# A scan and mixture-of-experts layer on one core: another order for the work ahead of the first scan

## The chip, the cores and the metric

The kernel runs on one core of a Trainium2 chip. A core has five engines that each work through their own list of instructions in order: TensorE (PE in the profile, with its weight loads as PEld), VectorE (DVE), ScalarE (ACT), GpSimd (POOL) and SyncE (SP, which here only issues DMAs). They meet through semaphores. Plain DMAs are issued by SP, DMAs with an index list (gathers and scatters) by POOL; both sorts run on the same 16 DMA engines, from two queues.

The metric is the device time of one execution in microseconds. The time before the change is the median of nine executions.

## The reference, cut to what matters

`x` is (2, 2048, 256): B = 2 batches of L = 2048 tokens with D = 256 values. Each token is normalised, and the output is the input plus two results on the normalised tokens:

```python
xn = _layernorm(x)
out = x + scan(xn, ...) + experts(xn, ...)

# scan: tokens of a batch are put in the order of their bucket (8 buckets), then a selective scan
buckets = argmax(l2norm(xn) @ l2norm(means).T)        # (2, 2048)
xs = xn in the stable order of buckets
delta = softplus(dt(x_proj(xs)) + bias); B, C from x_proj(xs) (+ a prompt of the bucket)
h = exp(delta * A) * h + delta * u * B                # 16 states for each of 256 channels
y = (h * C).sum(states) + D * u;  back to the old order

# experts: 8 experts with 256 -> 512 -> 256, each token goes to its two best
logits = xn @ w_gate; top two, softmax of the two: probs
out = sum over the two of probs * ((silu(xn @ w1[e]) * (xn @ w3[e])) @ w2[e])
```

All is float32.

## The kernel before, in words

**Front (lines 134 to 613).** Eight blocks of 512 tokens (`xts`) are loaded; ScalarE, TensorE and VectorE compute their statistics and their scores against the 8 bucket means and the 8 expert gates. `normalize` (L419) normalises each block in place and stores it into `xn_d` in DRAM, with four spare columns a row. `begin_sums` (L911) copies blocks of x into `acc_d`, the DRAM sum of the result (`acc<-in_x_dram`, 512 KB each). `choose` (L512) finds the two best experts of each token; `route` (L531) numbers the (token, expert) pairs by expert and cuts them into NT = 71 tiles of 128. To turn "pair to slot" into "slot to token" it calls `list_tokens` (L305): eight columns, each with two comparisons on VectorE (`one`, `num`), a product on VectorE and one on ScalarE, and 8 matmuls (L337) that add into one PSUM tile `pl`. A list `between` of closures is called after the columns: before the change `find_weights` (L569) after the second and `find_shares` (L589) after the fourth. `find_weights` computes which expert's weights each tile needs (`w_row`) and issues four weight fetches on POOL (tiles 0 and 1: `w13` of 1 MB and `w2` of 512 KB each). `find_shares` computes what each token gives to its two experts and stores that in the spare columns of `xn_d` in two DMAs of 2,048 runs of 16 bytes. From `pl` comes `token_of` (L613), the token of each slot; `load_rows` (L847) then gathers a tile's 128 tokens from `xn_d` (`xg_sb<-xn,token_of`). It waits for all stores to `xn_d`, those of the shares too.

**Sort (L437 to L497).** `sort_tokens` finds each token's bucket, counts with a scan, two triangular and ones matmuls (L462 to L465) and so on, and gives each token its place `pos` in the sorted order; it also finds where each bucket begins and ends (`first`, `last`, by way of the matmul `po`, L482). `list_rows` (L499) turns `pos` into `line_of` with `list_tokens` of two columns. `small_weights` (L273) prepares `diag`, `cp` (by the matmul `pc`) and `na`. When `front.close()` has freed the front's memory, tile 2's weights get a place there (`w13_2`, `w2_2`) and are fetched.

**Pieces and steps.** The scan of a batch goes in four pieces of 512 sorted tokens, eight in all. A piece gathers its rows on POOL (`gather`, `xs<-xn,line_of`, four gathers), transposes them (`turn`), projects them (`project`, `end_projection`: matmuls `px`), stores B and C and loads them back broadcast (`load_b`, `load_z`), finds the step size (`step_size`: matmul `pd`, then three ScalarE activations) and a softplus by four factors (`square` on ScalarE and `series` on VectorE, called for all i by `first_series` in the first piece). A step is four states of half the channels: four products (`bu`, L766) and four scans (`hs`, L775) on VectorE, the decays (`da`) on ScalarE, then transposes and small matmuls on TensorE. There are 64 steps.

**Expert parts.** A tile's work is cut in three parts, `part_up(t, 0)`, `part_up(t, 1)` (16 matmuls each, L875) and `part_down(t)` (8 matmuls, L898, then a scatter-add on POOL): 213 parts. `silu` and `gate` are the tile's VectorE work; they are written two places after their part. `turn` (L854) transposes a tile's rows and computes `own`, the token's share (L862, L866).

**The order** of each engine's instructions is that of the text: the last lines tie each instruction to the one before on its engine. `lead` (L1000) is the hand-written order until the first scan: with each of its 13 entries goes one expert part and then the entry's links of the first piece's chain. From there a planner gives out parts between the steps: each of VectorE's and TensorE's works has a cost, and a part is given when TensorE's sum falls behind VectorE's times one ratio, so that the parts end 16 scans ahead of the last. At the end `out_dram<-acc` copies the sum and the last piece is added to it.

Of the kernel before, what the change touches and what calls it, by code (L numbers as in the profile page):

```python
# [40 lines left out]
F32 = mybir.dt.float32  # L41
# [8 lines left out]
P = 128  # L50
# [12 lines left out]
def scan_moe_kernel(  # L63
# [373 lines left out]
    def sort_tokens():  # L437

        sc = sml.tile([P, BJ, K], F32, tag="sc", name="sc")
        for b in range(B):  # L440
            nc.vector.tensor_tensor(
                sc[:, b * J : (b + 1) * J, :], of_batch(b)[:, :, 0:K],
                m_scale.unsqueeze(1).to_broadcast([P, J, K]), ALU.mult,
            )
        bm = sml.tile([P, BJ], F32, tag="bm", name="bm")
        bk = sml.tile([P, BJ], F32, tag="bk", name="bk")
        first_of_max(sc, bm, bk)
        oh = sml.tile([P, BK, J], F32, tag="both", name="oh")
        nc.vector.tensor_tensor(
            oh.rearrange("p (b k) j -> p b k j", b=B), idx_m.rearrange("p (b k) j -> p b k j", b=B),  # L450
            bk.rearrange("p (b j) -> p b j", b=B).unsqueeze(2).to_broadcast([P, B, K, J]),
            ALU.is_equal,
        )
        cum = sml.tile([P, BK, J], F32, tag="cum2", name="cum")
        nc.vector.tensor_tensor_scan(
            cum.rearrange("p k j -> p (k j)"), keep.rearrange("p k j -> p (k j)"),
            oh.rearrange("p k j -> p (k j)"), 0.0, ALU.mult, ALU.add,
        )
        tot = sml.tile([P, BK], F32, tag="tot", name="tot")
        nc.vector.tensor_copy(tot, cum[:, :, J - 1])  # L460
        pn = ps_m.tile([P, 2 * BK + B], F32, tag="m", name="pn")
        nc.tensor.matmul(pn[:, 0:BK], lhsT=before, rhs=tot, start=True, stop=True)  # L462
        nc.tensor.matmul(pn[:, BK : 2 * BK], lhsT=ones, rhs=tot, start=True, stop=True)
        for b in range(B):
            nc.tensor.matmul(  # L465
                pn[0:K, 2 * BK + b : 2 * BK + b + 1], lhsT=tot[:, b * K : (b + 1) * K],
                rhs=ones[:, 0:1], start=True, stop=True,
            )
        cnt = sml.tile([P, BK], F32, tag="cnt", name="cnt")
        nc.vector.tensor_copy(cnt, pn[:, BK : 2 * BK])  # L470
        base = sml.tile([P, BK], F32, tag="base", name="base")
        for b in range(B):
            own = slice(b * K, (b + 1) * K)
            nc.vector.tensor_tensor_scan(
                base[:, own], ones[:, 0:K], cnt[:, own], 0.0, ALU.mult, ALU.add
            )
        nc.vector.tensor_sub(base, base, cnt)
        nc.vector.scalar_tensor_tensor(base, base, -1.0, pn[:, 0:BK], ALU.add, ALU.add)
        cntT = sml.tile([K, B], F32, tag="cntT", name="cntT")
        nc.vector.tensor_copy(cntT, pn[0:K, 2 * BK : 2 * BK + B])  # L480
        po = ps_m.tile([K, B], F32, tag="m", name="po")
        nc.tensor.matmul(po, lhsT=before[0:K, 0:K], rhs=cntT, start=True, stop=True)  # L482
        fst = sml.tile([K, B], F32, tag="fst", name="fst")
        nc.vector.tensor_copy(fst, po)
        nc.vector.tensor_tensor(cum, cum, over(base, J), ALU.add)
        nc.vector.tensor_mul(cum, cum, oh)
# [443 lines left out]
    for k in range(n_x // 2, n_x):  # L930
        begin_sums(k)
# [46 lines left out]
    def turn_tile(t: int):  # L978
        tiles[t].turn()
        if t + NW < NT:  # L980
            tiles[t + NW].load_rows()
# [187 lines left out]
```

## Time and profile before

| | us |
|---|---|
| median of 9 executions | 795.65 |
| lowest and highest | 792.78 and 796.36 |
| the profiled execution, its own time | 797.61 |
| its span, first to last instruction | 795.8 |

| engine | busy us | share of the span |
|---|---|---|
| PE | 715.5 | 90% |
| DVE | 711.1 | 89% |
| ACT | 508.6 | 64% |
| POOL | 522.2 | 66% |

How to read it: all times of the views are microseconds from the span's start. A timeline row gives the start, the busy time, the engine, the line, the operation, `out<-in`, the size, and in brackets the idle time before it and what is taken to have ended that idle time; rows that follow each other on a line are merged (x7). SPq marks DMA issues of SP. A wait for several semaphores is put down to the last one that the profile shows from an engine, which may not be the real one. PEclk is the granted share of TensorE's clock.

### The profile page before, as it was taken

The page shows a single profiled execution, that of the slowest core. Times are in us where ns is not written, and L with a number is a line of the kernel's source. Part 1 is how long each engine was busy: PE and PEld are TensorE (multiplying, and loading weights), DVE is VectorE, ACT ScalarE, POOL GpSimd, SP SyncE. Part 2 cuts the span into 40 slices and gives each one's busy share as a digit, 9 for nine tenths or more (in the row PEclk, how much of TensorE's full clock was granted, in tenths as well). Part 3 has the DMA queues.
Part 4 walks back from the last instruction along what each step waited for, and adds up shares of the span by engine and source line. Part 5 has one row for each costly group of instructions (what it writes and reads, how often), then busy time and mean ns, then how long its engine had stood idle before and what let it go on. Part 6 is the DMA issues. An engine that isn't in the chain of part 4 may idle for free.

```text
span 795.8 us, 16967 instructions
## 1 busy us (share of the span) xinstructions
PE 715.5 (90%) x6552; PEld 608.3 (76%) x6552; DVE 711.1 (89%) x1162; ACT 508.6 (64%) x986; POOL 522.2 (66%) x374
## 2 busy tenths in 40 slices
PE   7385979899999999899999999999899998999972
PEld 5145768589878998699868986898679886998752
DVE  8866279899999999899989999899799998999991
ACT  4821266585669666776677666866687577766671
POOL 2023738667867786688868886788668887687303
PEclk9656999999999999999999999999999999999986
DMA  9593354754368547664775468537744855444362
GB/s 283 216 321 114 58 172 107 233 157 93 103 157 261 137 107 209 170 171 108 218 189 154 94 214 228 132 57 241 205 109 127 275 162 113 107 105 97 80 218 27
DMA packets 61215, 125.90 MB, mean 158 GB/s; under 512 B 24464, under 2 KB 42032, under 8 KB 53776
## 3 DMA queue, kind: packets, MB, share of 16 engines
q0 software_dynamic: 40224, 65.03, 34.2%
q1 hardware_dynamic: 20912, 59.80, 22.9%
q8 instruction: 52, 0.85, 0.4%
q14 instruction: 27, 0.22, 0.1%
HBM read 180.06 MB, written 27.00 MB: 260 GB/s over the span
## 4 chain that ended last, share of the span: by engine, by line
PE 66%; ACT 6%; DMA 5%; DVE 3%; issue 3%; POOL 2%; POOLq 0%; SPq 0%; ACTq 0%; DVEq 0%
PE p_ps L875 28%; PE py L898 14%; PE pt_s L787 11%; PE y L796 6%; ACT ht L791 2%; DMA out_dram<-acc 2%; PE pt_g L858 2%; PE y L728 1%; PE px L655 1%; DMA xs<-xn,line_of 1%; PE pd L692 1%; DVE hs L775 1%; POOL acc L816 1%; DVE bu L766 1%; DMA acc<-yo,token_of 1%
## 5 line engine op out<-in xcount | busy, mean ns | idle before, releaser
L875 PE MATMUL p_ps<-xT,w 128*128 128x128 f32 x2272 | 281.6, 280 | 5.3 <-ACT sq L702 4.3
L875 PEld LDWEIGHTS p_ps<-xT,w 128*128 128x128 f32 x2272 | 269.7, 195 | 20.2 <-issue 9.2
L775 DVE TENSOR_TENSOR_SCAN hs<-da,carry,bu 128x512 f32<-128x512 f32 x192 | 245.8, 1281 | 0.0
L760 ACT ACTIVATE da<-dl,na 128x512 f32<-128x512 f32 x256 | 182.0, 723 | 1.0 <-DVE hs L775 1.0
L816 POOL DMA_INDIRECT acc<-yo,token_of x71 | 136.0, 1916 | 67.5 <-ACT yo L902 18.5
L766 DVE TENSOR_TENSOR bu<-du,bt 128x512 f32<-128x512 f32 x256 | 173.5, 678 | 0.0
L791 ACT COPY ht<-pt_s 128x512 f32<-128x512 f32 x256 | 137.6, 591 | 33.1 <-PE pt_s L787 32.6
L787 PE MATMUL pt_s<-ident,hs 128*128 128x128 f32 x1024 | 140.5, 283 | 14.2 <-ACT ht L791 8.1
L898 PE MATMUL py<-w,g 128*128 128x256 f32 x568 | 138.0, 386 | 12.2 <-ACT r L696 8.7
L835 POOL DMA_INDIRECT w<-in_w_up_dram,w_row x71 | 94.0, 1324 | 83.2 <-DVE w_row L584 36.7
L787 PEld LDWEIGHTS pt_s<-ident,hs 128*128 128x128 f32 x1024 | 120.0, 145 | 31.2 <-ACT ht L791 15.1
L898 PEld LDWEIGHTS py<-w,g 128*128 128x128 f32 x568 | 103.4, 192 | 26.9 <-ACT r L696 10.3
L849 POOL DMA_INDIRECT xg_sb<-xn,token_of x71 | 91.7, 1291 | 37.7 <-DVE tot L460 16.3
L835 POOL DMA_INDIRECT w<-in_w_down_dram,w_row x71 | 93.7, 1320 | 21.6 <-issue 12.8
L883 ACT ACTIVATE t_sb<-p_ps 128x512 f32<-128x512 f32 x71 | 42.6, 600 | 69.3 <-PE p_ps L875 69.0
L902 ACT ACTIVATE yo<-py,own 128x256 f32<-128x256 f32 x71 | 33.9, 477 | 79.4 <-PE py L898 79.3
L775 DVE TENSOR_TENSOR_SCAN hs<-da,bu 128x512 f32<-128x512 f32 x64 | 78.2, 1222 | 0.0
L796 PE MATMUL y<-ht,z 128*32 128x128 f32 x2048 | 73.5, 277 | 2.5 <-ACT ht L791 1.9
L796 PEld LDWEIGHTS y<-ht,z 128*32 128x32 f32 x2048 | 50.6, 109 | 24.2 <-issue 13.2
L816 POOL DMA_INDIRECT acc<-yt,line_of x28 | 54.7, 1955 | 21.0 <-issue 10.4
L888 DVE SCALAR_TENSOR_TENSOR t_sb<-t_sb,p_ps 128x512 f32<-128x512 f32 x71 | 48.1, 677 | 11.2 <-ACT t_sb L883 10.9
L892 DVE SCALAR_TENSOR_TENSOR g<-t_sb,p_ps 128x512 f32<-128x512 f32 x71 | 48.2, 679 | 9.0 <-PE p_ps L875 6.5
(188 smaller groups left out, 633.0 us busy)
## 6 DMA issues: line engine op xcount, KB each, us to landing
bt<-bc SPq DMA_DIRECT2D x32, 1024.0 KB, 5.2
z<-bc SPq DMA_DIRECT2D x32, 256.0 KB, 3.5
xn<-xt SPq DMA_DIRECT2D x8, 520.0 KB, 2.6
xt<-in_x_dram SPq DMA_DIRECT2D x8, 512.0 KB, 6.9
acc<-in_x_dram SPq DMA_DIRECT2D x8, 512.0 KB, 6.5
w<-in_w_up_dram,w_row POOLq DMA_INDIRECT x71
w<-in_w_down_dram,w_row POOLq DMA_INDIRECT x71
xg_sb<-xn,token_of POOLq DMA_INDIRECT x71
```

The source lines that it names most:

```text
L760: nc.scalar.activation(self.da[i], self.piece.dl[:, self.h, :], AF.Exp, scale=na[:, self.h, n : n + 1])
L766: nc.vector.tensor_mul(self.bu[i], self.piece.du[:, self.h, :], self.piece.bts[self.q][:, i, :])
L775: nc.vector.tensor_tensor_scan(self.hs[:, :, i], self.da[i], self.bu[i], start, ALU.mult, ALU.add)
L787: nc.tensor.transpose(pt[:, j, :], self.hs[:, t0 : t0 + G, :].rearrange("p t n -> p (t n)"), ident)
L791: nc.scalar.copy(self.ht[i], pt)
L796: nc.tensor.matmul(p.ys[self.h][j * G : (j + 1) * G, i, :], lhsT=p.zs[q][:, i * (P // G) + j, :], rhs=self.ht[i][:, j, :], start=False, st ...
L816: ins = nc.gpsimd.indirect_dma_start(out=to, out_offset=bass.IndirectOffsetOnAxis(ap=numbers, axis=0), in_=rows, in_offset=None, compute_o ...
L835: nc.gpsimd.indirect_dma_start(out=to[self.t % NW], out_offset=None, in_=rows, in_offset=bass.IndirectOffsetOnAxis(ap=w_row[:, self.t : se ...
L849: nc.gpsimd.indirect_dma_start(out=self.xg, out_offset=None, in_=xn_d, in_offset=bass.IndirectOffsetOnAxis(ap=token_of[:, self.t : self.t ...
L875: nc.tensor.matmul(p[:, f, :], lhsT=wk[:, h, f * P : (f + 1) * P], rhs=self.xT[:, h, :], start=h == 0, stop=h == ND - 1,)
L892: nc.vector.scalar_tensor_tensor(self.g, self.s, 0.5, self.p3, ALU.mult, ALU.mult)
L898: nc.tensor.matmul(py, lhsT=self.g[:, f, :], rhs=w2[:, f, :], start=f == 0, stop=f == NH - 1)
```

## The change

It moves work in the front and in `lead`; no operation is added or taken away, and all data stay the same.

1. **Shares first.** `find_shares` is called after the list's second column, `find_weights` after the third. The last four `begin_sums` are called behind `route` and `load_rows`, so SP issues the last `xn_d` store and both share stores ahead of them.
2. **Sort in the list.** `sort_tokens` is cut into `choose` (buckets), `count` (counts and matmuls `pn`), `place` (up to `pos`) and `bound` (matmul `po`, then `first` and `last`). `choose` comes after the list's fifth column, `count` after the seventh, `place` after `load_rows`; `list_rows(0)` comes right after the first expert part, and `bound`, `small_weights`, `front.close()` and the fetches of tile 2's weights behind it. `own` (now `find_share`) is written after both tiles' transposes.
3. **Lead.** `lead` has 12 entries, so 12 expert parts: the turns, the projection and both step sizes stand together, and the two series are cut in halves.

```diff
@@ route
-            [lambda: None, find_weights, lambda: None, find_shares],
+            [lambda: None, find_shares, find_weights, lambda: None, sort.choose, lambda: None, sort.count],
@@ Sort.bound: the end of what was sort_tokens, without place
+            po = ps_m.tile([K, B], F32, tag="m", name="po")
+            nc.tensor.matmul(po, lhsT=before[0:K, 0:K], rhs=self.cntT, start=True, stop=True)
+            fst = sml.tile([K, B], F32, tag="fst", name="fst")
+            nc.vector.tensor_copy(fst, po)
+            for b in range(B):
+                nc.vector.tensor_scalar(first[b], begins, fst[:, b : b + 1], None, ALU.add)
+                nc.vector.tensor_scalar(last[b], first[b], self.cntT[:, b : b + 1], None, ALU.add)
@@ the order of the front
-    for k in range(n_x // 2, n_x):
-        begin_sums(k)
     route()
     for t in tiles[:NW]:
         t.load_rows()
-    pos = sort_tokens()
-    diag, cp = small_weights()
-    front.close()
...
-    tiles[NW - 1].load_up()
-    tiles[NW - 1].load_down()
+    for k in range(n_x // 2, n_x):
+        begin_sums(k)
+    sort.place()
@@ turn_tile
         tiles[t].turn()
+        if t > 1:
+            tiles[t].find_share()
@@ before lead
-    def first_series(h: int):
-        for i in range(len(LOG1P) + 2):
+    def first_series(h: int, steps):
+        for i in steps:
...
+    tiles[0].find_share()
+    tiles[1].find_share()
+    jobs[0]()
+    list_rows(0)
+    sort.bound()
+    diag, cp = small_weights()
+    front.close()
...
+    tiles[NW - 1].load_up()
+    tiles[NW - 1].load_down()
+    half = len(LOG1P) // 2 + 1
+    early, rest = range(half), range(half, len(LOG1P) + 2)
     lead = [
-        [lambda: list_rows(0, pos)], [p.gather], [], [], [], [lambda: p.turn(0)],
-        [lambda: p.turn(1), p.find_members],
+        [], [p.gather], [], [], [lambda: p.turn(0), lambda: p.turn(1), p.find_members],
         [lambda: p.project(0), lambda: p.project(1), p.end_projection],
-        [lambda: p.load_b(0), *(lambda q=q: p.load_z(q) for q in range(NQ)), lambda: p.step_size(0)],
-        [lambda: p.step_size(1), lambda: first_series(0)], [lambda: first_series(1)],
-        [lambda: p.begin(0), lambda: p.begin(1)], [lambda: p.mask_z(0)],
+        [
+            lambda: p.load_b(0), *(lambda q=q: p.load_z(q) for q in range(NQ)),
+            lambda: p.step_size(0), lambda: p.step_size(1),
+        ],
+        [lambda: first_series(0, early)], [lambda: first_series(0, rest)],
+        [lambda: first_series(1, early)], [lambda: first_series(1, rest), lambda: p.begin(0)],
+        [lambda: p.mask_z(0), lambda: p.begin(1)],
     ]
```

## The prediction

> **What bounds the kernel now.** I read the chain of waits by engine first, then busy time by stage (columns: PE, PEld, DVE, ACT, POOL, granted PE clock, DMA share, GB/s).
>
> ```profile
> PE 66%; ACT 6%; DMA 5%; DVE 3%; issue 3%; POOL 2%; POOLq 0%; SPq 0%; ACTq 0%; DVEq 0%
> ...
> 36.00:64.00 28.00, 17.09 (x65) 9.29 (x65) 20.54 (x57) 9.24 (x17) 4.37 (x4) 0.50 0.82 264
> 64.00:88.00 24.00, 18.75 (x131) 17.66 (x132) 12.50 (x47) 4.19 (x10) 13.32 (x14) 0.76 0.37 117
> 88.00:116.00 28.00, 22.22 (x125) 16.70 (x124) 12.10 (x23) 15.26 (x28) 12.34 (x11) 0.94 0.51 144
> 116.00:752.00 636.00, 612.60 (x5873) 532.74 (x5871) 608.94 (x890) 437.81 (x858) 478.57 (x315) 0.99 0.58 154
> ```
>
> From 116 to 752 both PE and DVE are 96% busy: nothing of that stage changes. So the change is worth how much earlier the first scan starts, less what work of the front is carried past it. Until then a single chain counts: token list, first tile's rows, sort's list, the piece's gather, its links. The timeline shows it, POOL and SP first, then DVE and PE:
>
> ```profile
> 41.99 0.51 SPq L432 DMA_DIRECT2D xn<-xt  x1
> 47.47 8.70 SPq L602 DMA_DIRECT2D xn<-share  x2
> ...
> 64.46 0.97 POOL L849 DMA_INDIRECT xg_sb<-xn,token_of  x1 [16.32 <-DVE tot L460]
> ...
> 70.00 1.00 POOL L835 DMA_INDIRECT w<-in_w_up_dram,w_row  x1 [2.06 <-DVE na L289]
> 71.31 1.01 POOL L835 DMA_INDIRECT w<-in_w_down_dram,w_row  x1 [0.30 <-DVE v L313]
> ...
> 79.66 1.00 POOL L835 DMA_INDIRECT w<-in_w_up_dram,w_row  x1 [4.80 <-PE p_ps L875]
> 80.97 0.95 POOL L620 DMA_INDIRECT xs<-xn,line_of  x1 [0.31 <-issue]
> ```
> ```profile
> 53.64 0.46 DVE L325 TENSOR_TENSOR num<-idx_p,f 128x568 bf16<-128x568 bf16 x1 [2.69 <-DMA xn<-xt]
> ...
> 60.09 0.23 DVE L613 SCALAR_TENSOR_TENSOR token_of<-tokens,none 128x71 int32<-128x71 f32 x1
> ...
> 104.13 0.69 DVE L713 SCALAR_TENSOR_TENSOR dl<-sq,e 128x512 f32<-128x512 f32 x1 [13.77 <-ACT sq L702]
> ```
> ```profile
> 54.95 4.28 PE L337 MATMUL pl<-num,one 128*128 128x142 bf16 x16 [1.36 <-ACT num L331]
> ...
> 109.35 3.53 PE L875 MATMUL p_ps<-xT,w 128*128 128x128 f32 x16 [4.34 <-ACT sq L702]
> ```
>
> The token list is ready at 60.3, yet the first rows' gather goes at 64.46. DVE's `tot` is no operand of it: the real wait is the second share store, begun at 53.6 (the last of the merged 8.70) with 9.9 us to landing, so 63.5. Why 9.9? The packet counts say it: 3,638 packets under 512 B moved between 57 and 60, and 464 in the nine us before, while the weights' 3 MB went. The small runs stand behind the weights.
>
> **Part 1, shares first.** Shares take 1.9 us of DVE (45.43 to 47.35) and now follow column 2: 39.8 to 41.7. Without the copies ahead, the last `xn` store goes at 39.4, after the one before; the stores land about 2 us apart, so near 43.5. The two share stores then need some 3.4 us (4,096 packets at the rate of 57 to 60): landed by about 47, long before the list. The wait for them goes. What is late next is the list itself.
>
> The weights are fetched 3.3 us later (w_row at 45.8; was 42.5) and now beside the last four copies, 2 MB. The copies took 41.3 to 49.8, the weights 48.3 to 58.6 with 0.5 MB of stores. One after the other that is some 17.5 us from 46.5: 64. The first tile's gather is issued before that and its packets come 1.7 us after issue, so this just hides; each us that DMA is slower costs one. [...]
>
> **Part 2, sort between the columns.** DVE has room in the list: a column is 1.45 us of DVE, but 2.13 of PE (4.27 for two). Added are `choose`, 2.3 us (60.24 to 62.55), and `count`, 1.4 (62.58 to 63.94); the stall of 2.69 for a store goes. From 36.8: two columns 39.8, shares 41.7, column 43.2, weights' rows 45.8, two columns 48.7, `choose` 51.0, columns 52.5 and 54.0, `count` 55.3, last column. The sixth column's factors reach PE at 52.9 through ACT; then PE binds: three columns of 2.13 and `pn`, 1.25 (63.99 to 65.2), end at 60.5. From there 1.1 us to the list: 61.6, 1.3 later than now. The gather follows at 61.9 (POOL went 0.3 after `w_row`): **2.5 us earlier** than 64.46. `place` runs beside the gather's 2.8 us and is hidden; without that cover it costs 2.6. The first part and `list_rows` have the same order as before: `line_of` starts at 74.1 instead of 76.6.
>
> **A new wait.** POOL's order is tile 2's two fetches, tile 3's, then the piece's gather. The first waits for `na`, now behind the list: `bound`, `diag`, `cp` and `na` take 2.0 us (68.25 to 69.91 and 0.35 for `fst`), so 76.2. Then 76.3, 77.6, 78.9 and the gather at 80.2. That is only **0.8** ahead of 80.97: POOL takes 1.7 of the 2.5. Queued behind are tile 4's fetch and rows, needed much later.
>
> **Part 3, lead.** The last gather lands 2.75 after its issue (84.73 to 87.48): 86.7. Until `xd` (95.64) stand now a part, the turn, a down part and the projection: 8.2 us. After: the second turn 0.9, one part 2.0, projection 3.0: 5.8. That is **2.4**. From `xd` to the first `sq` 7.7 now; after it a part 2.05, both `pd` 2.2, a down part 2.4 and `yo` 0.5: 7.2, **0.5**. From `sq` to the first scan 13.5 now (103.38 to 116.93). After: 12 series links of 0.76, `gate` twice, `silu`, `own`, `z` (2.9), two `bu` (1.2) and 0.7 to the first link: 13.9 or so, **0.4 lost**. First scan 3.3 earlier, at 113.6.
>
> Carried past it: one `silu`, 0.6 of DVE. On PE the thirteenth part ended at 116.6; it now ends near 114.0. So DVE is 2.7 ahead and PE 2.6.
>
> **Sum:** 2.5 - 1.7 + 2.4 + 0.5 - 0.4 - 0.6 = 2.7, by PE 2.6; I take 2.6. The profiled execution took 797.6, so 795.0; it lies 2.0 above the median, and the median comes to 795.65 - 2.6 = 793.05, say **793.0**.
>
> **Unknown costs.** The trace shows no piece gather behind three fresh fetches: between nothing (POOL's cadence of 1.3 us is all) and 1.6 us (the fetches' 1.5 MB moved 71.7 to 77.1, then the gather's packets); I take nothing, since the last gather is issued after that. Nor a list with `pn` inside: between 1.3 later (taken) and as now.
>
> The clock is the third. Half clock makes a part 3.53 instead of 2.05. In this trace clock changes stand on a grid of 3.41 us; from full clock, a stretch with PE busy 50% or less is followed by half, one with 58% or more is not. PE will idle some 2.4 us before the last gather lands and 2.3 while a `gate` waits behind the series: each between nothing and 1.7. I take nothing, the rows nearest: 102.8 to 106.2 with 58% kept full clock. [...]
>
> **Rivals.** (a) *Nothing to measure*: one or two windows at half clock (1.7 each) or DMA a us slower, 793.9 to 795.7. [...] (b) *More*: list as early as now and POOL's fetches not held by `na` (they need only the front's memory): 1.3 and 1.6 more, 790.1. Against: `na` ended 0.09 ahead of the fetch at 70.00. (c) *Slower*: the planner has one more part to place, and some parts move by half a step. At a piece's border PE already stands once for 3.1 us (`py` at 331, behind ACT's step sizes), then its part runs at half clock (3.46 instead of 1.9): 4.7 together. One such stall more gives 797.7. It decides from the point where a part falls behind the step sizes in PE's order. Against: the parts' places are the same in the second half. (d) The order of the DMAs could fail to free the gather, if the small runs are slow alone too: over 15 us for both stores. The 1,800 a us after the weights speak against it; I give it no chance of its own.
>
> **Chances.** Forecast 0.48 (791.5 to 794), (a) 0.26, (b) 0.12, (c) 0.14. A measurement of this kernel tells about 0.2% from no change, 1.6 us: faster 0.60, same 0.26, slower 0.14. Range 789.8 to 797.2: (b) and nearly all of (a), with the part of (c) that a half stall gives.
>
> **What would show it.** The shares landed before the list ends, and POOL's first row gather right after `token_of`, near 62; the list's end near 61.6; the piece's first gather near 80.2 and right behind three fetches; `xd` near 92.5; the first scan near 113.6. Wrong if the row gather still waits for a DMA, if the clock is half between 85 and 104, or if the scans start 3 us earlier and the end does not follow.

## The result, and the profile after

| | before | after |
|---|---|---|
| median of the runs | 795.25 (31) | 806.12 (10) |
| lowest and highest | 792.52 and 798.35 | 802.12 and 812.27 |
| the profiled execution, its own time | 797.61 | 806.72 |
| its span | 795.8 | 804.6 |
| first scan, last scan | 116.9, 777.3 | 117.0, 786.0 |

The ratio after to before is **1.0147**, 95% interval 1.0127 to 1.0167: 1.5% slower, where 0.3% faster was forecast, and outside the range. Ratios here and below are the record's and leave out executions more than 1.5% above the fastest of their kernel; the two medians of the table alone give 1.0137. The profiled execution of before lies 2.4 above its median, so the profiles show 8.8 of the medians' 10.9. The first scan did not come earlier, and the 256 scans took 8.6 us longer from the first to the last (669.0; before 660.4).

The chain's shares and the busy times by stage, after (columns as before the change: PE, PEld, DVE, ACT, POOL, granted PE clock, DMA share, GB/s):

```profile
PE 68%; ACT 7%; DMA 4%; DVE 3%; issue 3%; POOL 1%; POOLq 0%; SPq 0%; ACTq 0%; DVEq 0%
...
36.00:64.00 28.00, 17.90 (x72) 10.35 (x72) 22.25 (x65) 8.57 (x14) 6.70 (x7) 0.50 0.85 244
64.00:88.00 24.00, 16.85 (x103) 15.05 (x103) 9.37 (x35) 3.60 (x9) 10.49 (x12) 0.72 0.39 130
88.00:116.00 28.00, 24.76 (x137) 19.13 (x138) 11.91 (x22) 14.45 (x26) 13.42 (x11) 0.88 0.47 141
116.00:752.00 636.00, 611.19 (x5792) 531.93 (x5791) 600.54 (x881) 434.34 (x851) 476.19 (x314) 0.98 0.57 152
```

The last row holds the loss. In the same 636 us VectorE got 600.54 of work done where it was 608.94, and PE ran 5,792 matmuls where it was 5,873; PE is as busy as before (611.2 to 612.6), with the clock at half for 30.7 of the 636 us (before 10.2). VectorE waited 13.9 in all for `t_sb` and 12.3 for the squares (before 6.7 and 9.9).

The front after the change, from the timelines of SP and POOL, then of VectorE and PE:

```profile
36.45 2.76 SPq L432 DMA_DIRECT2D xn<-xt  x3
41.31 1.74 SPq L614 DMA_DIRECT2D xn<-share  x2
43.10 3.18 SPq L927 DMA_DIRECT2D acc<-in_x_dram  x4
...
61.09 0.97 POOL L861 DMA_INDIRECT xg_sb<-xn,token_of  x1 [10.07 <-DVE cnt L477]
...
77.57 1.00 POOL L847 DMA_INDIRECT w<-in_w_up_dram,w_row  x1 [8.61 <-DVE cp L280]
78.88 1.01 POOL L847 DMA_INDIRECT w<-in_w_down_dram,w_row  x1 [0.30 <-issue]
80.19 0.99 POOL L847 DMA_INDIRECT w<-in_w_up_dram,w_row  x1 [0.30 <-issue]
81.49 0.96 POOL L632 DMA_INDIRECT xs<-xn,line_of  x1 [0.30 <-issue]
```
```profile
60.58 0.23 DVE L625 SCALAR_TENSOR_TENSOR token_of<-tokens,none 128x71 int32<-128x71 f32 x1
...
104.44 0.69 DVE L725 SCALAR_TENSOR_TENSOR dl<-sq,e 128x512 f32<-128x512 f32 x1 [12.18 <-ACT sq L714]
```
```profile
95.36 1.98 PE L704 MATMUL pd<-xd,dtT 32*128 32x512 f32 x4
97.83 0.63 PE L870 MATMUL pt_g<-ident,xg_sb 128*128 128x128 f32 x2 [0.50 <-ACT r L708]
99.51 3.78 PE L913 MATMUL py<-w,g 128*128 128x256 f32 x8 [1.04 <-ACT r L708]
```

The row gather goes 0.3 behind `token_of`, 3.4 earlier than before (64.46): the wait for the shares is gone. The piece's gather goes at 81.49, later than before (80.97), the fourth of POOL's row behind three fetches. And between the second step size and the first square stands `py`, late and at half clock (3.78 for 8 matmuls; 1.99 at full clock).

Where the scans lose: the distance of the same scan, after less before, is 0.1 at scan 0, 0.6 at scan 12, 7.4 at scan 24, 6.8 at scan 44, 11.2 at scan 52, 13.2 at scan 80, then down to 6.4 at scan 168 and up to 8.7 at the last. Two places. At the first, `list_rows(1)` (the second batch's list of rows, `pl`) is made beside the scans. PE there, before:

```profile
145.50 1.07 PE L655 MATMUL px<-u,xpT 128*64 128x512 f32 x2
146.69 0.65 PE L337 MATMUL pl<-num,one 128*128 128x32 bf16 x8
148.75 0.65 PE L337 MATMUL pl<-num,one 128*128 128x32 bf16 x8 [1.41 <-ACT num L331]
149.22 2.03 PE L875 MATMUL p_ps<-xT,w 128*128 128x128 f32 x16
151.18 1.07 PE L660 MATMUL px<-member,cp 8*64 8x512 f32 x2
```

and after, with VectorE's row that pays for it:

```profile
145.48 1.07 PE L667 MATMUL px<-u,xpT 128*64 128x512 f32 x2
147.00 0.66 PE L337 MATMUL pl<-num,one 128*128 128x32 bf16 x8 [0.45 <-ACT num L331]
149.07 0.64 PE L337 MATMUL pl<-num,one 128*128 128x32 bf16 x8 [1.41 <-ACT num L331]
150.23 0.66 PE L870 MATMUL pt_g<-ident,xg_sb 128*128 128x128 f32 x2 [0.52 <-PE pl L337]
151.35 3.78 PE L913 MATMUL py<-w,g 128*128 128x256 f32 x8 [0.46 <-ACT xT L872]
155.06 1.96 PE L672 MATMUL px<-member,cp 8*64 8x512 f32 x2
156.95 3.78 PE L890 MATMUL p_ps<-xT,w 128*128 128x128 f32 x16
```
```profile
161.40 0.69 DVE L903 SCALAR_TENSOR_TENSOR t_sb<-t_sb,p_ps 128x512 f32<-128x512 f32 x1 [5.00 <-ACT t_sb L898]
```

Behind the list stands a down part (`pt_g`, `py`) where before an up part (`p_ps`) stood. From 149.1 the clock is half for 13.7 us, `py`, `px` and `p_ps` take 3.78, 1.96 and 3.78 (at full clock 1.99, 1.07 and 2.03), and VectorE stands 5.00. The second place is the next piece's step sizes:

```profile
250.06 1.12 PE L704 MATMUL pd<-xd,dtT 32*128 32x512 f32 x2
251.12 1.08 PE L808 MATMUL y<-ht,z 128*32 128x128 f32 x32
252.13 1.12 PE L704 MATMUL pd<-xd,dtT 32*128 32x512 f32 x2
253.18 0.44 PE L870 MATMUL pt_g<-ident,xg_sb 128*128 128x128 f32 x2
256.75 3.78 PE L913 MATMUL py<-w,g 128*128 128x256 f32 x8 [3.13 <-ACT r L708]
```

`py` stands behind both `pd` and waits 3.13 for ScalarE's step sizes, then runs at half clock (3.78). Before, that down part stood between the two `pd` and did not wait:

```profile
241.76 1.12 PE L692 MATMUL pd<-xd,dtT 32*128 32x512 f32 x2
242.81 1.08 PE L796 MATMUL y<-ht,z 128*32 128x128 f32 x32
243.82 0.44 PE L858 MATMUL pt_g<-ident,xg_sb 128*128 128x128 f32 x2
244.24 1.99 PE L898 MATMUL py<-w,g 128*128 128x256 f32 x8
246.24 1.12 PE L692 MATMUL pd<-xd,dtT 32*128 32x512 f32 x2
```

### The profile page after: what moved, and what is told of

Same layout as the page of the kernel before. It is cut to its first block, busy times and chain, and to the rows that moved or that the text cites. A ratio compares the mean times of both kernels' runs of the same rounds, so it can differ in the third digit from the quotient of the medians.

```text
span 804.6 us, 16964 instructions
## 1 busy us (share of the span) xinstructions
PE 723.3 (90%) x6552; PEld 615.2 (76%) x6552; DVE 709.7 (88%) x1162; ACT 508.9 (63%) x986; POOL 525.1 (65%) x374
## 4 chain that ended last, share of the span: by engine, by line
PE 68%; ACT 7%; DMA 4%; DVE 3%; issue 3%; POOL 1%; POOLq 0%; SPq 0%; ACTq 0%; DVEq 0%
PE p_ps L890 28%; PE py L913 15%; PE pt_s L799 12%; PE y L808 6%; DMA out_dram<-acc 2%; PE pt_g L870 2%; ACT ht L803 2%; PE px L667 1%; PE y L740 1%; DVE hs L787 1%; DMA xs<-xn,line_of 1%; ACT da L772 1%; PE px L672 1%; ACT sq L714 1%; ACT e L707 1%
## 5 line engine op out<-in xcount | busy, mean ns | idle before, releaser
L890 PEld LDWEIGHTS p_ps<-xT,w 128*128 128x128 f32 x2272 | 271.2, 196 | 17.9 <-issue 10.5
L828 POOL DMA_INDIRECT acc<-yo,token_of x71 | 138.8, 1955 | 71.7 <-ACT yo L917 35.7
L803 ACT COPY ht<-pt_s 128x512 f32<-128x512 f32 x256 | 137.8, 590 | 32.9 <-PE pt_s L799 32.4
L913 PE MATMUL py<-w,g 128*128 128x256 f32 x568 | 143.0, 397 | 12.9 <-ACT r L708 8.9
L799 PEld LDWEIGHTS pt_s<-ident,hs 128*128 128x128 f32 x1024 | 121.6, 147 | 30.7 <-ACT ht L803 13.1
L913 PEld LDWEIGHTS py<-w,g 128*128 128x128 f32 x568 | 106.7, 198 | 29.3 <-ACT r L708 10.5
L861 POOL DMA_INDIRECT xg_sb<-xn,token_of x71 | 93.4, 1315 | 33.3 <-issue 13.4
L847 POOL DMA_INDIRECT w<-in_w_down_dram,w_row x71 | 91.2, 1285 | 21.6 <-issue 13.4
```

The lines of the kernel that those rows point to most:

```text
L799: nc.tensor.transpose(pt[:, j, :], self.hs[:, t0 : t0 + G, :].rearrange("p t n -> p (t n)"), ident)
L803: nc.scalar.copy(self.ht[i], pt)
L828: ins = nc.gpsimd.indirect_dma_start(out=to, out_offset=bass.IndirectOffsetOnAxis(ap=numbers, axis=0), in_=rows, in_offset=None, compute_o ...
L847: nc.gpsimd.indirect_dma_start(out=to[self.t % NW], out_offset=None, in_=rows, in_offset=bass.IndirectOffsetOnAxis(ap=w_row[:, self.t : se ...
L861: nc.gpsimd.indirect_dma_start(out=self.xg, out_offset=None, in_=xn_d, in_offset=bass.IndirectOffsetOnAxis(ap=token_of[:, self.t : self.t ...
L890: nc.tensor.matmul(p[:, f, :], lhsT=wk[:, h, f * P : (f + 1) * P], rhs=self.xT[:, h, :], start=h == 0, stop=h == ND - 1,)
```

## The experiments

Two theories. **The parts' order**: `lead` has 12 entries in place of 13, so each tile's pattern of up, up, down is one place on beside every later link of a piece's chain. **The front**: what the new front leaves on POOL and the DMA queues is paid for later. The runs came in five groups, each beside the kernel before, which took 793.7 in the first group and 808.9, 806.4, 803.0 and 808.3 in the others, on other chips or at other times (the first and the third on the same chip); so kernels are compared by their ratio to it and not by their times. For each profile I also give two stretches of scans: from scan 8 to scan 24 (the list of the second batch stands there) and from scan 44 to scan 56 (the second piece's step sizes). These can be set beside each other across the groups: e11 below is the kernel before once more, in a group where it takes 806.4, and its two stretches are 47.2 and 32.0 as in the first profile.

**First group: the two parts of the change alone** (before: 793.7).

`e1_thirteen`, the changed kernel with an empty entry at the end of `lead`:

```diff
-        [lambda: p.mask_z(0), lambda: p.begin(1)],
+        [lambda: p.mask_z(0), lambda: p.begin(1)], [],
```

> The changed kernel with a thirteenth expert part before the first scan (one empty entry at the end of lead). Theory 1, the parts' places: with 12 parts ahead, a down part instead of an up part stands beside batch 1's list (147 to 157 in the changed trace) and beside the step sizes (253 to 260), PE idles and drops to half clock. Then this kernel loses that: first scan some 2 us later than the changed kernel's 117.0, but scan 48 no more than 1 us behind the first scan's shift, and 796 to 799 in all. Theory 2, the front itself (what it leaves on the DMAs and POOL) delays the later stage: then it stays at 805 or more.

`e2_twelve`, the kernel before with its last two entries joined:

```diff
-        [lambda: p.begin(0), lambda: p.begin(1)], [lambda: p.mask_z(0)],
+        [lambda: p.begin(0), lambda: p.begin(1), lambda: p.mask_z(0)],
```

> The kernel before with its last two entries of lead joined: 12 parts ahead of the first scan, front untouched. Theory 1: it loses in the stage of the scans as the changed kernel does, some 7 to 9 us there, with a half clock stretch near 150; first scan 1 to 2 us earlier; 801 to 804. Theory 2: 793 to 796, since its front is that of before.

`e3_old_lead`, the changed front with the 13 entries of the kernel before (its first one empty, since the list is made earlier):

```diff
+        [], [p.gather], [], [], [], [lambda: p.turn(0)],
+        [lambda: p.turn(1), p.find_members],
```

> The changed front with the lead of before, 13 parts in the old places. Theory 1: no loss after the first scan. The row gather lands 0.4 us earlier than before and the piece's gather goes 0.5 later than before, so first scan at 117 to 118 and 795 to 797 in all. Theory 2: 803 or more.

`e4_shares`, the kernel before with part 1 alone:

```diff
-            [lambda: None, find_weights, lambda: None, find_shares],
+            [lambda: None, find_shares, find_weights],
...
+    for k in range(n_x // 2, n_x):
+        begin_sums(k)
```

> The kernel before with one part of the change alone: shares after the list's second column, weights after the third, the last four copies behind them; sort and lead as before. The row gather is issued 1 to 3 us earlier than 64.46; but as in the changed trace the copies and weights end near 66 instead of 59, so the first rows land near 66.5 (before 67.2). Theory 1 and 2 differ little here: theory 1 gives 793.5 to 796 (13 parts, at most 1 us won), theory 2, if the later copies are what disturbs the scans, 800 or more.

| | ratio to before (95%) | first scan | scans 8 to 24 | scans 44 to 56 |
|---|---|---|---|---|
| before | 1 | 116.9 | 47.2 | 32.0 |
| after | 1.0147 (1.0127, 1.0167) | 117.0 | 54.3 | 36.7 |
| e1_thirteen | 1.0030 (1.0013, 1.0048) | 115.9 | 47.2 | 32.0 |
| e2_twelve | 1.0163 (1.0115, 1.0211) | 115.4 | 51.1 | 36.3 |
| e3_old_lead | 1.0026 (1.0004, 1.0048) | 115.7 | 47.2 | 32.0 |
| e4_shares | 1.0001 (0.9981, 1.0020) | 115.6 | 47.2 | 32.0 |

The loss goes with the number of parts and not with the front: one empty entry takes away four fifths of it, and the old front with twelve parts has all of it. In e2's profile the first scan comes 1.5 *earlier* than before, and both stalls are there. The front theory falls. The new front is worth 0.2% at most: e4's first scan is 1.4 earlier in the profile, and the interval of its time just holds that; e1 and e3 are 0.3% slower with the first scan 1.0 and 1.2 earlier. Their profiles show no reason for that (e1's profiled execution was its fastest, 793.0); it stays open.

**Second group: the front further, and fifteen parts** (before: 808.9).

`e5_copies_late`, e1 with the last four copies held behind the first tiles' rows:

```diff
+        tc.add_manual_dep(begin_sums(k), tiles[1].turned.name, after, reason="behind the weights")
```

> The version with thirteen parts ahead of the first scan (first scan at 115.9 in its profile), and besides it the last four of the copies that preset the sums, 2 MB, wait for ScalarE's copy of the first transposed rows, so that nothing but the weights' 3 MB stands ahead of the first rows. In the thirteen-part run the rows were issued at 61.2 and landed at 65.0, a microsecond after the weights' last packet at 64.0. Theory 'the rows wait for the 5 MB ahead of them': the weights end near 59 to 60, the rows land 2.0 to 2.8 after their issue (62.5 to 63.5 if the issue stays near 61), the piece's list comes 1.5 to 2 earlier, at about 72.3, and the first scan 1 to 2 earlier; the time is 0.1 to 0.25% below the thirteen-part version's 796.0, so 794 to 795. Rival 'the weights alone bind, the copies cost nothing': rows land within 0.4 of 65, first scan within 0.4 of 115.9, time unchanged.

`e6_gather_first`, e5 with the piece's gather issued at once:

```diff
     list_rows(0)
+    p.gather()
     sort.bound()
```

> The run before with the piece's row gathers issued on GpSimd ahead of bound's work and of the fetches of tile 2's and tile 3's weights, right behind the list of the piece's rows. Theory 'POOL's fetches that wait for na hold the gather': with the list at about 72 to 74 the first gather goes within 0.6 of it instead of 6.0 later (74.02 to 80.02 in the thirteen-part run), the four gathers land by about 79 to 80 and PE's first link comes up to 5 earlier; the first scan 2 to 5 earlier than in the run before. Tile 2's weights come up to 4 later, near 84, which costs nothing if the part that needs them stands behind the turn. Rival 'PE and the clock set the first links': the gathers land earlier, but the copy of the second turn (87.1 in the thirteen-part run) moves by less than 1, and the time stays within 0.2% of the run before.

`e7_squares_first`, e6 with the first squares ahead of the down part:

```diff
-            lambda: p.step_size(0), lambda: p.step_size(1),
+            lambda: p.step_size(0), lambda: p.step_size(1), lambda: first_series(0, early),
```

> The run before, and besides the first half of the series of chunk 0 stands right behind the two step sizes, ahead of the down part that stood between; the series take one place less, and two empty places stand at the end, so that still thirteen parts are ahead of the first scan. Theory 'the way from the projection to the first square is lost to the down part': 10.2 us after, 9.8 with thirteen parts, 7.7 in the order before; now near 4.5 to 6, the first scan 3 to 5 earlier than in the run before, and since the places of the parts are those of before, the end follows in full: 0.4 to 0.6% below the run before, so 787 to 791. Rival 'the front's gain is eaten later': the first scan comes 3 or more earlier but the last scan by less than 1.5.

`e8_fifteen`, the kernel before with two empty entries:

```diff
-        [lambda: p.begin(0), lambda: p.begin(1)], [lambda: p.mask_z(0)],
+        [lambda: p.begin(0), lambda: p.begin(1)], [lambda: p.mask_z(0)], [], [],
```

> The kernel before with two empty places added at the end of the list ahead of the first scan: fifteen parts instead of thirteen; nothing else. A tile's three parts alternate (two up, one down), so fifteen has the order of twelve beside every later link. Theory 'the order of the parts beside the links decides': PE again stands and falls to half clock where a down part takes the place of an up part (near 150 and 255), and the time is 8 or more above before's, counted from the first scan, besides the two parts' own time being moved and not added: 802 or more. Rival 'one part fewer ahead of the scan is what costs, since it must be done beside the scans': two parts more help or cost at most their idle DVE time, first scan 4 later, and the time is within 0.5% of before's or up to 4 above it.

| | ratio to before (95%) | first scan | scans 8 to 24 | scans 44 to 56 |
|---|---|---|---|---|
| e5_copies_late | 0.9940 (0.9902, 0.9978) | 118.2 | 48.5 | 32.0 |
| e6_gather_first | 0.9854 (0.9787, 0.9921) | 115.5 | 53.1 | 32.0 |
| e7_squares_first | 0.9967 (0.9931, 1.0003) | 114.7 | 51.1 | 32.0 |
| e8_fifteen | 1.0050 (1.0009, 1.0090) | 128.4 | 55.8 | 33.8 |

e5: the weights ended at 59.0 and not at 64.0, but the rows were used only 0.7 earlier (`pt_g` at 64.31; e1 64.97): with the weights out, it still took 2.9 us from the gather's issue to the use of its rows. Neither theory's number: under half of the expected gain, and `line_of` came 0.15 earlier. What it is worth in time is not told, since e1 did not run beside it. e6: POOL's rows, from its repeat `e12_gather_again`, show the gather right behind the list (`line_of` at 73.56), six microseconds earlier than in e1:

```profile
74.00 0.95 POOL L632 DMA_INDIRECT xs<-xn,line_of  x1 [6.42 <-DVE fst L504]
...
77.77 0.95 POOL L632 DMA_INDIRECT xs<-xn,line_of  x1 [0.30 <-issue]
79.02 1.01 POOL L847 DMA_INDIRECT w<-in_w_up_dram,w_row  x1 [0.30 <-issue]
```

but PE first has the parts that stand ahead of the turn, and the copy of the turn comes at 85.3 there (e1 87.1): of six microseconds 1.8 arrive. Beside e5, which differs by this edit alone and ran in the same group, e6's gather goes 4.7 earlier (75.14, e5 79.87) and the copy of the turn comes 3.9 earlier (86.44, e5 90.30); but e5 stands in its front for the unexplained reason told at the end, so neither pair gives the edit's price by itself. e7: the first square came at 96.8 (e6 101.6), as expected, yet the scans only 0.8 earlier: cut in halves, the series' second squares stand behind a part's `t_sb` on ScalarE, and from the first square to the first scan it took 17.9 in place of 13.9. e8: fifteen parts lose, 8.6 in scans 8 to 24; since the first scan comes 11 later too, the time does not tell the two theories apart. Its order on PE does at the list: behind it stand `pt_g` and `py` again, as with twelve. At the second place fifteen is not twelve over again: an up part stands between the two `pd`, `py` behind them waits 0.43, and the stretch loses 1.8.

**Third group: the place of the list, and ten parts** (before: 806.4).

`e9_list_moved`, the changed kernel with the second batch's list seven scans later. `e11_list_moved_before` was meant as the control, but it is the kernel before without any edit and is read as that; so the list's later place with thirteen parts was not measured. The edit of e9:

```diff
-    at_place(2, 3, lambda: list_rows(1), 2.5, 4.0)
+    at_place(4, 2, lambda: list_rows(1), 2.5, 4.0)
```

> The changed kernel with one edit: the list of the second batch's rows is made seven scans later (step 4, place 2 in place of step 2, place 3), where by the planner's sums an up part and not a down part is what PE has beside it; still twelve parts ahead of the first scan. Theory 'a link that has a down part beside it stands and drops the clock': PE's row of half clock from 149 is gone, the scans' distance to the kernel before grows by less than 2 from scan 12 to scan 24 (in the changed kernel 0.6 to 6.9), the stall near 255 with both pd ahead of a down part stays (2.8), and the time is 4 to 6 below the changed kernel's: 800 to 802 where before's is 795. Rival 'with twelve parts some link always pays': the stall turns up beside the moved list or another link before scan 32, and the time stays within 2 of the changed kernel's.

> The kernel before with that same edit, the control: thirteen parts ahead of the first scan, and the list of the second batch's rows at step 4, place 2. There the parts beside it are an up part and then a down part, and beside its old place an up part. Theory 'only the neighbour counts': within 0.3% of before. Rival 'the later place is better for any order' (the list's work falls where VectorE has room): 3 or more below before.

`e10_ten`, e7 with whole series and no empty entries:

```diff
+            lambda: p.step_size(0), lambda: p.step_size(1), lambda: first_series(0, every),
+        ],
+        [lambda: first_series(1, every)],
+        [lambda: p.begin(0), lambda: p.begin(1)], [lambda: p.mask_z(0)],
```

> The version with the gathers first and the squares right behind the step sizes, with the two series whole again and no empty places: ten parts ahead of the first scan, the same place in the pattern of three as thirteen. Theory 'the place in the pattern decides, not the number': no stall at the list of the second batch, first scan near 109.5 to 111 (squares at 96.8 and the 13.5 from there that the kernel before takes), and the time within 0.5% of before's or under it: three parts more beside the scans cost PE 6.1, and the scans start 6 to 7 earlier. Rival 'every part fewer ahead of the scan costs': as twelve cost 1.5%, ten cost 3% or more, 815 and up where before's is 795.

> The version with the piece's gathers ahead of the fetches once more, unchanged, because it was measured at 0.985 of before with an interval of 0.979 to 0.992, while the next version, whose first scan came 0.8 earlier, had 0.997. Theory 'the gain is the early first scan's': at most 1.5 from the front, so 0.998 to 1.000 of before. Rival 'the gain is real and lies in the order of the parts beside the first piece': 0.985 to 0.992 again.

| | ratio to before (95%) | first scan | scans 8 to 24 | scans 44 to 56 |
|---|---|---|---|---|
| e11 (before) | 0.9966 (0.9908, 1.0024) | 121.7 | 47.2 | 32.0 |
| e9_list_moved | 1.0061 (1.0018, 1.0104) | 120.7 | 51.2 | 38.3 |
| e10_ten | 0.9886 (0.9809, 0.9963) | 110.5 | 48.0 | 32.4 |
| e12_gather_again | 0.9912 (0.9868, 0.9955) | 114.3 | 53.3 | 32.0 |

e9 lies between. At the old place nothing stands any more, but at the new one VectorE waits 2.88, and the clock is half from 171.5: the rival's picture. Scans 8 to 24 hold the list's own work in either case and take 4.0 more than before's, where the changed kernel takes 7.1 more; the time says the same, 1.0061. The second place stays (38.3), as expected. e10 bears out the pattern: ten parts, three fewer than thirteen, lose nothing at either place, and the first scan comes at 110.5, 13.6 behind the first square. "Every part fewer costs" falls. e12 repeats e6's gain (0.9912, its rival's number); by their profiles it does not come from scans 8 to 24, where both lose.

**Fourth group: a part inside the list** (before: 803.0).

`f1_part_between` gives two parts at the list, the down part ahead of it and the up part between its columns; the other three give one part between the columns (`f2_before_between` in the kernel before, `f3_gather_between` in e6, `f4_ten_between` in e10):

```diff
-    at_place(2, 3, lambda: list_rows(1), 2.5, 4.0)
+    at_place(2, 3, lambda: (give(), list_rows(1, [give])), 2.5, 4.0)
```

> The changed kernel (twelve parts ahead of the first scan); the down part that stood behind the list of the second batch's rows stands ahead of it, and the up part that came next stands between the list's two columns. Theory 'the list's neighbour': PE no longer idles 1.4 between the columns, nor before the down part; the half clock from 149 is gone, the scans' distance to the kernel before grows by less than 2 between scan 12 and scan 24 (changed kernel: 0.6 to 7.4); the time is 4 to 7 below the changed kernel's, 1.006 to 1.010 of before, the rest being the stalls from 253 on. Rival 'the list costs by itself': the distance still grows by 4 or more there and the time stays within 0.3% of the changed kernel's 1.0147.

> The kernel before with one expert part (an up part) between the two columns of the list of the second batch's rows; the control. In its trace PE idles 1.41 between the columns at full clock, and no stall follows. Theory 'the list costs only where the clock drops': within 0.25% of before. Rival 'the columns' gap costs always': 0.3% or more below before.

> The version with the piece's gathers first (measured at 0.985 and 0.991 of before), with an up part between the two columns of the second batch's list. In both its profiles the clock is half after that list (148.6 and 147.4) and the scans lose 5 to 6 between scan 12 and scan 20. Theory: that loss goes, the time is 0.4 to 0.7% below that of the version without, so 0.980 to 0.986 of before. Rival: the loss only moves, 0.988 to 0.992.

> The version with ten parts and the squares first (measured at 0.989), with an up part between the two columns of the second batch's list. In its profile no half clock follows that list, and the scans lose nothing between scan 12 and scan 20. Theory: within 0.3% of 0.989. Rival 'the columns' gap costs always': 0.985 or less.

| | ratio to before (95%) | first scan | scans 8 to 24 | scans 44 to 56 |
|---|---|---|---|---|
| f1_part_between | 1.0109 (1.0010, 1.0208) | 119.6 | 53.9 | 36.6 |
| f2_before_between | 0.9979 (0.9916, 1.0042) | 121.4 | 48.3 | 32.0 |
| f3_gather_between | 0.9917 (0.9877, 0.9957) | 115.9 | 48.6 | 32.0 |
| f4_ten_between | 0.9896 (0.9810, 0.9982) | 110.3 | 49.5 | 32.4 |

f1: with the down part *ahead* of the list the stretch still takes 53.9, now as a wait of 4.68 on VectorE for the list's first column, whose matmuls stand behind `py`. So my theory of the neighbour behind the list looks too narrow, as far as one profile tells: it is of f1's longest execution, 821.6, where the others took 807.3 to 817.1. In f3 the loss of 6 in scans 8 to 24 is down to 1.4, as expected, but the time did not follow: 0.9917, no better than without, and the number of its rival "the loss only moves". The profiles bear the rival out: against before, f3 loses 5.2 between scans 64 and 112, and g1, the same kernel, 5.1 between scans 128 and 160. f2 and f4 differ from the kernels they were made from by less than their intervals.

**Fifth group: the changed kernel and the best front side by side** (before: 808.3).

> The version with the piece's gathers first and an up part between the two columns of the second batch's list, once more, unchanged (0.9917 of before, where before took 803). Theory 'its own front is shorter': where before takes 794, it takes 0.995 to 0.999 of before; where before takes 803 or more, 0.988 to 0.995. Rival 'it only avoids the stand that before has in some calls': where before takes 794, 1.000 or more; 798 by its own time in either case.

> The changed kernel, unchanged, beside the same runs of before. Theory 'twelve parts lose beside the scans, whatever the front': 1.010 to 1.018 of before again, in either case. Rival 'where before stands in its front, the changed kernel's other front makes up for the loss': within 0.5% of before where before takes 803 or more.

g1 took 0.9955 (0.9896 to 1.0014), just above its theory's 0.988 to 0.995, and 804.5 by its own time where the rival had 798: neither is borne out. g2 took **1.0153** (1.0084 to 1.0222), with 53.7 and 38.6 in the two stretches and the same rows (`py` behind both `pd` with a wait of 3.13 at 262.49). So the changed kernel's loss is the same where the kernel before runs slower by itself. Of the versions with the gather first, five measurements (e6, e12, f3, e10, f4) have their interval below 1, and two (e7, g1) touch it; e5, which does not have it first, lies below 1 too. All are from groups where before takes 803 to 809. None ran where before takes 794, and their own times (795.9 to 805.5) are no better than that: that they beat it there is not shown.

## Why the prediction was wrong

**The step that failed first: "nothing of that stage changes".** It set everything beside the scans aside and counted only how early they start. But `lead` hands the planner one part more, and the parts come in a pattern of three. In all fourteen profiles with 13 or 10 parts scans 44 to 56 took 32.0 to 32.4; in all five with 12 (after, e2, e9, f1, g2) 36.3 to 38.6; in the one with 15, 33.8. That much is shown. Half of it the prediction had in its hands: rival (c) named the mechanism, "behind ACT's step sizes", and its price of 4.7; measured, 36.7 less 32.0 is 4.7 (that it agrees to the tenth is luck: over the five profiles with 12 parts it is 4.3 to 6.6). It was given 0.14 on the ground that "the parts' places are the same in the second half". The half that was read, late in the list of parts, does not tell which part stands beside a link in the first pieces. The order of the two kernels on PE beside each `pd` would have told it without a run.

**No rival had the list.** The stretch from scan 8 to 24 cost 7.1 (54.3 less 47.2), more than the other. With 4.7 that makes 11.8; 3.1 of it is made up by the last scan, which leaves the 8.7.

How much the list costs goes with **the clock**. By the half-clock time between scans 8 and 24, in all twenty profiles: with none the stretch took 47.2 to 48.3; with 3.4 us 48.5 to 51.1; with 6.8 us 51.2; with 10.2 us 53.7 and 53.9; with 13.7 us 53.1 to 55.8.

The prediction's edge, half clock at 50% and full at 58%, was right for the trace it was read from and did not hold beyond it. On the grid of 3.41 us, counted from each profile's own half-clock stretches (after's from 60 to 700 us begin 0, 7, 22, 53, 145 and 177 steps of 3.41 behind 74.05), this is PE's busy share in the window that holds the gap between the list's columns (the emptier one where the gap lies across two), worked out from the PE rows, and what followed, for the fifteen profiles without a part between the columns:

| | busy in the window | the clock then |
|---|---|---|
| before, e10, e4, e1 | 59%, 59%, 61%, 62% | full |
| e3, e11 | 68%, 75% | full |
| e5 | 61% | half |
| e6, e12 | 57%, 55% | half |
| after, g2, e2, e8, e9, e7 | 46%, 47%, 38%, 42%, 20%, 0% | half |

But for e5 these part between 57% and 59%. Two other falls of the changed kernel do not fit at all: the window ahead of the half clock from 97.9 was 85% busy, and the one ahead of the half clock from 255.0, at the second place, 61%. e1 shows a window at the list that is kept:

```profile
145.65 0.67 PE L337 MATMUL pl<-num,one 128*128 128x32 bf16 x8
147.74 0.66 PE L337 MATMUL pl<-num,one 128*128 128x32 bf16 x8 [1.41 <-ACT num L331]
148.21 2.03 PE L890 MATMUL p_ps<-xT,w 128*128 128x128 f32 x16
150.17 1.07 PE L672 MATMUL px<-member,cp 8*64 8x512 f32 x2
```

The window there is 146.4 to 149.8; PE works from 147.74 on, 2.1 of 3.41. e6 and e12 have the same order of instructions with the scans 0.4 and 1.6 earlier, the gap falls otherwise on the grid, and they lose 5.9 and 6.1 in scans 8 to 24; e5, of that order too, loses 1.3. So even thirteen parts were safe by luck at this place; what twelve add is a down part whose matmuls wait another 0.52 and 0.46 right after the gap. Nor does the length of a single gap part them: e7 has one of 3.95, in the other fourteen no gap of PE there is over 2.5, and the clock was half in eight of these. That the list costs 4.0 and 6.7 with twelve parts where it is moved (e9) or the down part is put ahead of it (f1) is not explained by its neighbour behind alone; what it is, stays open.

**Part 1** was right in its order and wrong in its cover. The shares landed at 46.4 (forecast about 47) and the wait went. But "this just hides" fell: the weights ended at 66.0 (forecast 64), the gather's first packets moved at 64.3, 3.2 behind its issue and not 1.7, and the rows were used at 66.97, only 0.4 earlier than before. The weights stood ahead of them on POOL's queue; the last 8 KB packet of these began at 64.4, the last of 4 KB ended at 66.0. In e5, with the weights out by 59.0, the 1.7 came back.

**Part 2**: the token list was ready at 60.8, 0.8 earlier than worked out, and the row gather went at 61.09. `line_of` came at 75.48, forecast 74.1: that lateness is the rows', used only at 66.97.

**A new wait** was right: POOL's order, `na` and three fetches at a cadence of 1.3 are the rows above, and the gather 6.0 behind the list. It cost 0.5 against before in place of gaining 0.8, because the list was late. What it hid is told with e6: with the gather ahead the turn came 1.8 earlier than in e1 and 3.9 earlier than in e5.

**Part 3**: from the first turn's copy to `xd` 5.1 against 7.75 before, the 2.4 of the forecast and a bit more. From `xd` to the first square, "7.2", was **10.2**. The sum had the durations, that of `yo` ahead of the squares too, and left out that `py`, behind both `pd`, waits for ScalarE's `r` of the second (1.04) and then runs at half clock (3.78 where 1.99 is full). It is the stall of rival (c) once more, in the lead itself. With the old lead (e3) it was 7.7. From the first square to the first scan 13.3, forecast 13.9. First scan 117.0, forecast 113.6: 1.0 up to `xd` (93.48, forecast 92.5), 3.0 from there to the first square, 0.6 won back behind it.

**The clock**, "I take nothing": half from 74.0 and from 97.9, 6.8 each (before, 3.4 each from 75.5 and from 109.6). The second is a sign of being wrong that the prediction had named.

And the forecast's whole gain, 2.6, is 0.3%: against the 11.8 of the two places it would not have shown.

## What to carry to other kernels

Where hand-placed work alternates with a repeating pattern, one piece more or less ahead shifts the pattern beside everything that follows; print the two orders on the bounding engine beside every link before you price the front. The changed kernel's PE, 96% busy over 636 us of the scans, was at half clock for 30.7 of them, in stretches of 3.4 to 13.7 us; so price each idle place by the window of 3.41 us that holds it: in the twenty profiles 158 of the 258 windows at full clock that were under 70% busy were followed by half clock, and 13 of the 3,739 others. And an early issue is worth only what the next engine's work ahead of it leaves: of six microseconds at the gather 1.8 arrived against one kernel, of 4.7 3.9 against another.

## What was not expected of the hardware

In these runs no share of busy time is an edge for the clock. With a part between the list's columns it fell to half in f3, g1 and f4 after windows with 77%, 60% and 85% by the same count, for 3.4 us, and stayed full in f2 after 64%. Over all twenty profiles, in the windows at full clock from the first change of the clock behind 60 us on: at 50% or less, 140 of 143 were followed by half clock; between 50% and 70%, 18 of 115; at 70% or more, 13 of 3,739. What decides in between, these traces do not show.

The copies of 32 KB a packet, begun right behind the 16-byte stores, took 5.1 us each on the mean for the 13 packets begun between 46.1 and 47.3 (1.8 before, where they ran ahead of those stores). The weights' first packet moved at 54.4, ahead of the last copy packet (begun at 56.8); before, at 48.3, behind it (47.5).

In the third group the kernel before stands in its front for something that the profile does not show. ScalarE in e11, which is that kernel:

```profile
82.86 0.37 ACT L860 COPY xT<-pt_g 128x256 f32<-128x256 f32 x1 [2.19 <-PE pt_g L858]
86.43 0.47 ACT L902 ACTIVATE yo<-py,own 128x256 f32<-128x256 f32 x1 [3.20 <-PE pt_u L641]
91.47 0.60 ACT L883 ACTIVATE t_sb<-p_ps 128x512 f32<-128x512 f32 x1 [4.57 <-PE pt_u L641]
```

`py` ended at 83.8 and `p_ps` at 85.6, so neither released these; the copy of the turn came at 91.97 where it was 87.89, and the first scan at 121.7 where it was 116.9. Every later profile whose gather is not first has that copy at 90.3 to 93.4; those with the gather first have it at 85.3 to 86.4. How much of their 1% is only that, stays open. Nor is the front all of it: e11's distance to the first profile of before is 4.8 at the first scan, still 4.9 at scan 64, and 13.2 at the last, so 8.3 of it came beside the scans, in the same kernel.
